# Output products of a two-layer graph attention kernel as seven products of halves, added in place

## The chip, the cores and the metric

The kernel runs on one core of a Trainium2 chip. The metric is the device time of one execution in microseconds (us); lower is better. All data are float32.

## What is computed

The input x holds 128 graphs of 128 nodes with 512 features, adj a boolean adjacency matrix per graph. Two layers follow each other, each an attention over the adjacency with a residual and a layer norm:

```python
# --- layer 0: 4 heads of 64, no norm ahead of the projections ---
q, k, v = x @ Wq, x @ Wk, x @ Wv                    # split into heads
sim  = where(adj, q k^T * 64**-0.5, -float32_max)
x    = layernorm(x + softmax(sim) v @ Wo + bo)
# --- layer 1: 8 heads of 64, layer norm (gamma, beta) ahead of the projections ---
h    = layernorm(x) * gamma + beta
q, k, v = split(h @ w_qkv.T)
sim  = where(adj | eye, q k^T * 64**-0.5, -1e9)
x    = layernorm(x + softmax(sim) v @ w_out.T + b_out)
```

The matrix of attended values that the output product multiplies (called aT here, turned) is 256 wide in layer 0 and 512 wide in layer 1; the output is 512 wide in both.

## The kernel before

**Groups and steps.** The graphs are handled in 64 groups of two ("batches" b = 0 and 1). `step(s)` is a software pipeline written out by hand: at step s it makes the query, key and value products of layer 0 for group s (`product_0`), the softmax of layer 0 for group s - 1, the query and key products of layer 1 for group s - 2 (`p("qk", ...)`), and V and the softmax of layer 1 for group s - 3 (`p("v", ...)`). A step has two halves; half b works on batch b of the softmax groups: `scores` (TensorE), the mask and the row maximum (VectorE), the exponentials (ScalarE), `normalised` (GpSimd), `blocks` (VectorE turns blocks of 32 x 32), a trip through DRAM that completes the transposition (`put`, `fetch`), and `attend` half a step later.

**Order.** The schedule is manual: each engine executes its instructions in the order in which `step` calls the functions, and waits where an operand or a buffer is not ready. `scores` puts the exponentials of its layers into `waiting` and issues layer 0's at once; layer 1's are issued by the next call of `exponentials()`. Copies out of PSUM on ScalarE and adds out of PSUM on VectorE stand in the same queues as the softmax. DMAs are issued from SP, in order too.

**Seven products.** The projections of two batches are already made as one 2 x 2 block product with seven products of halves (the Winograd form of Strassen's scheme) in place of eight. GpSimd makes the sums of the inputs (`sums`), the weights' sums are made once. The seven products go into three accumulators, as this table says (product: accumulator, whether it starts it):

```python
    INTO = {1: ("a", True), 2: ("c", True), 6: ("a", False), 5: ("f", True), 7: ("a", False),
            4: ("a", False), 3: ("f", False)}
```

So products 1, 6, 7 and 4 add into one PSUM bank one after the other, and the bank's partial sums are read out in between: after 1 and 6 by a ScalarE copy (L330, L371), after 7 by a VectorE add (L335, L376), after 4 by a ScalarE copy. A product that adds into the bank waits until the read-out before it is done. Products 5 and 3 share a second bank in the same way.

**Output products.** `residual` makes them for one batch at a time, undivided: two (layer 0) or four (layer 1) chunks of 128 with 512 columns (L493), one VectorE add to the residual (L499), the statistics, and the norm (`norms`, L524, VectorE for both layers) when `flush()` is called. Each float32 matmul shows as two records in the profile.

**PSUM.** Eight banks: five in turn for everything called `mm_tile` (scores take four at a time), and one each for `a`, `a0` and a shared `f`.

Of the kernel before, what the change touches and what calls it, by code (L numbers as in the profile page):

```python
# [18 lines left out]
D = 64  # L19
# [8 lines left out]
def kernel(ctx: ExitStack, tc: tile.TileContext, x, adj, wq, wk, wv, wo, bo,  # L28
# [13 lines left out]
    four = ctx.enter_context(tc.tile_pool(name="four", bufs=4))  # L42
    dram = ctx.enter_context(tc.tile_pool(name="dram", bufs=2, space=bass.MemoryType.DRAM))
    ps_mm = ctx.enter_context(tc.tile_pool(name="ps_mm", bufs=5, space=PSUM))
# [20 lines left out]
    X, M = {}, {}  # L65

    def load(g):
        if g >= NG:
            return
        X[g] = four.tile([P, G, E], F32, tag="x", name=f"x_{g}")  # L70
        M[g] = four.tile([P, G, N], U8, tag="m", bufs=6, name=f"m_{g}")
        nc.sync.dma_start(X[g], x[g * G:(g + 1) * G].rearrange("b n e -> n b e"))
        nc.sync.dma_start(M[g], adj[g * G:(g + 1) * G].rearrange("b i j -> i b j"))
# [8 lines left out]
    mhalf = const.tile([P, 2], F32, name="mhalf")  # L82
# [25 lines left out]

    spare = []
    for tag, n in (("qk1", 4), ("v1", 2), ("xT1", 2), ("xs1", 2)):  # L110
        rows_n = one.tile([P, n, E], F32, tag=tag, name=f"raw_{tag}")
        spare.extend(rows_n[:, i] for i in range(n))

    def load_transposed(dst, src, name, scaled=0):
        rows, cols = src.shape
        raws = []
        for r in range(rows // P):
            if not spare:
                raw = three.tile([P, cols], F32, tag="h", bufs=7, name=f"{name}_{r}")
            else:  # L120
                raw = spare.pop(0)
            nc.sync.dma_start(raw, src[r * P:(r + 1) * P, :])
            raws.append(raw)
# [36 lines left out]
    def weight_sums():  # L160
        for w, ws in ((w1qk, wsqk), (w1v, wsv)):
            for c in range(KH):
                if w is w1qk:
                    b11, b12 = w[:, c, :, 0], w[:, c, :, 1]
                    b21, b22 = w[:, KH + c, :, 0], w[:, KH + c, :, 1]
                else:
                    b11, b12 = w[:, c, 0], w[:, c, 1]
                    b21, b22 = w[:, KH + c, 0], w[:, KH + c, 1]
                t2, t3, t4 = ws[:, 0, c], ws[:, 1, c], ws[:, 2, c]
                nc.vector.tensor_sub(t3, b22, b12)  # L170
                nc.vector.tensor_sub(b12, b12, b11)
                nc.vector.tensor_sub(t2, b22, b12)
                nc.vector.tensor_sub(t4, b21, t2)

    def weight_sums_0():
        b11, b12, b21, b22 = (w0[:, c:c + KH, h].rearrange("p c t f -> p c (t f)")
                              for c in (0, KH) for h in range(2))
        t2, t3, t4 = (ws0[:, i].rearrange("p c t f -> p c (t f)") for i in range(3))
# [4 lines left out]

    weight_sums_0()
    load_transposed(w1, w_qkv, "w_qkv", scaled=INNER[1])
    setup.append(turn_gamma_beta)
    load_transposed(wo1, w_out, "w_out")
    setup.append(weight_sums)

    WO = (wo0, wo1)  # L190
    RATIO, H, XT, QK, V, QKV = {}, {}, {}, {}, {}, {}
# [14 lines left out]
    TURNED, SCR, RAW = {}, {}, {}  # L206

    def turn(l, g, b):
        if not 0 <= g < NG:
            return  # L210
        if b == 0:
            TURNED[l] = one.tile([P, 4, G * KC * 32], F32, tag=f"turned{l}", name=f"turned{l}_{g}")
        src = X[g][:, b] if l == 0 else H[g, b]
        nc.vector.transpose(TURNED[l].rearrange("p a (b c i) -> p a b c i", b=G, c=KC)[:, :, b],
                            src.rearrange("p (c a i) -> p a c i", a=4, i=32))
        if b == G - 1:
            SCR[l] = put(TURNED[l], f"scr{l}_{g}")

    def arrive(l, g):
        if not 0 <= g < NG:  # L220
            return
        RAW[l] = one.tile([P, 4, G, KC, 32], F32, tag=f"raw{l}", name=f"raw{l}_{g}")
        fetch(RAW[l].rearrange("p a b c i -> p a (b c i)"), SCR[l])

    def first_transposed():
        xT = XT[0, 0] = one.tile([P, KC, T], F32, tag="xT0", name="xT0_0")
        for b in range(G):
            pt = mm_tile(f"xt_{b}")
            for c in range(KC):
                nc.tensor.transpose(pt[:, c * N:(c + 1) * N], X[0][:, b, c * P:(c + 1) * P], ident)  # L230
# [26 lines left out]
    def sums(l, g):  # L257
        xT = XT[l, g]
        xs = one.tile([P, 4, KH, N], F32, tag=f"xs{l}", name=f"xs{l}_{g}")
        a = xT.rearrange("p (h c) (b n) -> p b h c n", h=2, b=2)  # L260
# [6 lines left out]
        XS[l, g] = xs  # L267
# [69 lines left out]
    def product_0(g, *which):  # L337
# [5 lines left out]
        for i in which:  # L343
# [10 lines left out]
            elif first:  # L354
                tag = {"a": "a0", "f": "f"}[bank]
                ACC[0, bank] = ps_st.tile([P, 512], F32, tag=tag, name=f"{bank}0_{g}")
# [11 lines left out]
            if i in (1, 5, 6):  # L368
                e = one.tile([P, 512], F32, tag=("e5_0" if i == 5 else f"e{i}"), name=f"e0_{i}_{g}")
                EV[0, i] = e[:, :3 * P]  # L370
# [8 lines left out]
    SM, SUM, PT, AT, XB = {}, {}, {}, {}, {}  # L379
# [56 lines left out]
    def blocks(k):  # L436
# [7 lines left out]
        pT = one.tile([P, 4, sum(HEADS), 32], F32, tag="pT", name=f"pT_{k}")  # L444
# [13 lines left out]
    def attend(k):  # L458
        both = members(k)
        if not both:  # L460
            return
        for l, g, b in both:
            K = HEADS[l] // 2
            pT = PT.pop((l, g, b))
            pm = mm_tile(f"av{l}_{g}_{b}")

            for h in range(HEADS[l]):
                s, kk = h % 2, h // 2
                o = pm[s * D:(s + 1) * D, kk * N:(kk + 1) * N]
                v = QKV[g][:, b, kk, 2, s * D:(s + 1) * D] if l == 0 else V[1, g][:, b, h * D:(h + 1) * D]  # L470
                nc.tensor.matmul(o.rearrange("p (a r) -> p a r", r=32), v, pT[:, :, s * K + kk, :],  # L471
                                 start=True, stop=True)
            AT[l, g, b] = two.tile([P, INNER[l]], F32, tag=f"aT{l}", name=f"aT{l}_{g}_{b}")
            nc.scalar.copy(AT[l, g, b], pm[:, :INNER[l]])  # L474

    def addend(l, k):

        for _, g, b in [m for m in members(k) if m[0] == l]:
            if l == 0:
                xin = X[g][:, b, :]  # L480
            else:
                xin = H.pop((g, b))
                nc.scalar.activation(xin, xin, AF.Copy, scale=RATIO.pop((g, b)))  # L483
            nc.gpsimd.tensor_tensor(xin, xin, (bias0, bias1)[l], op=ALU.add)  # L484
            XB[l, g, b] = xin

    def residual(l, k):
        for _, g, b in [m for m in members(k) if m[0] == l]:
            aT = AT.pop((l, g, b))
            nk = INNER[l] // P  # L490
            pm = mm_tile(f"o{l}_{g}_{b}")
            for c in range(nk):
                nc.tensor.matmul(pm, aT[:, c * P:(c + 1) * P], WO[l][:, c, :],  # L493
                                 start=(c == 0), stop=(c == nk - 1))
            if l == 0:
                y = three.tile([P, E], F32, tag="h", bufs=7, name=f"h_{g}_{b}")
            else:
                y = two.tile([P, E], F32, tag="y", name=f"y_{g}_{b}")
            nc.vector.tensor_add(y, pm, XB.pop((l, g, b)))  # L499
            st = three.tile([P, nc.vector.BN_STATS_DIM], F32, tag="st", name="st")  # L500
            nc.vector.bn_stats(st, y)
            mv = three.tile([P, nc.vector.BN_AGGR_DIM], F32, tag="mv", name=f"mv{l}_{g}_{b}")
            nc.vector.bn_aggr(mv, st)
            n = 2 - l
            ve = three.tile([P, 2], F32, tag="ve", name="ve")
            nc.gpsimd.tensor_scalar_add(ve[:, 0:1], mv[:, 1:2], EPS)  # L506
            if l == 0:


                nc.gpsimd.tensor_scalar(ve[:, 1:2], mv[:, 1:2], 1.0 + EPS, EPS * EPS,  # L510
                                        op0=ALU.mult, op1=ALU.add)
            r = three.tile([P, 2], F32, tag="rstd", name="rstd")
            nc.gpsimd.tensor_tensor(r[:, :n], ve[:, :n], mhalf[:, :n], op=ALU.pow)  # L513
            if l == 0:

                ratio = three.tile([P, 1], F32, tag="ratio", bufs=10, name=f"ratio_{g}_{b}")
                nc.gpsimd.tensor_scalar(ratio, ve[:, 1:2], r[:, 0:1], r[:, 1:2], op0=ALU.mult,
                                        op1=ALU.mult)
                RATIO[g, b] = ratio
            later.append(lambda: norms(l, g, b, y, mv, r))  # L520

    def norms(l, g, b, y, mv, r):
        n = 1 - l
        nc.vector.tensor_scalar(y, y, mv[:, 0:1], r[:, n:n + 1], op0=ALU.subtract, op1=ALU.mult)  # L524
        if l == 0:
            H[g, b] = y
        else:
            nc.sync.dma_start(out[g * G + b], y)


    def step(s):
# [6 lines left out]
        k = 2 * s  # L538
        scores(k)
        addend(0, k - 1)  # L540
        residual(1, k - 2)
        p("qk", 4, g=s - 3)
        exponentials()
        attend(k - 1)
        normalised(k)
        addend(1, k - 1)
        flush()
        turn(0, s + 1, 0)
        turn(0, s + 1, 1)
        product_0(s, 1, 5)  # L550
        p("", g=-1)
        blocks(k)
        arrive(0, s + 1)
        product_0(s, 2, 6)
        p("", g=-1)
        product_0(s, 3)
        residual(0, k - 1)
# [72 lines left out]
```

## Time and profile before

| | |
|---|---|
| median of 3 runs | 2984.99 us (2981.91 to 2985.11) |
| the profiled execution | 2984.46 us, its span 2982.7 us |
| TensorE busy | 2920.0 us, 98% |
| VectorE busy | 1854.0 us, 62% |
| GpSimd busy | 1567.4 us, 53% |
| ScalarE busy | 1334.2 us, 45% |
| granted TensorE clock, mean | 0.994 |

In the profile, PE is TensorE's matmuls, PEld its weight loads (which overlap with them), DVE is VectorE, ACT ScalarE, POOL GpSimd and SP the engine that issues the DMAs. A line of the timeline gives the start, the length, the engine, the line of the kernel, the operation, the tiles (out<-in), the shapes and the number of instructions merged; in brackets the idle time before it and what ended it. Matmuls are pipelined, so the durations of two neighbours overlap and only the difference of two starts is a cost.

### The profile page before, as it was taken

What the parts mean: (1) busy time and instruction counts of PE and PEld (TensorE: products, weight loads), DVE (VectorE), ACT (ScalarE), POOL (GpSimd) and SP (SyncE); (2) the same over time, 40 slices, a digit from 0 to 9 for tenths busy, and PEclk for the clock granted to TensorE, in tenths of its full rate; (3) what the DMA queues carried; (4) which work ended last, traced back from release to release, by engine and by line L of the source; (5) the groups of instructions that cost most, each with busy time, mean ns of one, the idle gap of its engine ahead of it and who ended that gap; (6) DMA issues with size and microseconds to landing.
All of it is one profiled execution on the core that took longest, in us unless ns stands there. A gap on an engine that the chain in (4) does not pass through costs nothing.

```text
span 2982.7 us, 59421 instructions
## 1 busy us (share of the span) xinstructions
PE 2920.0 (98%) x22089; PEld 2402.9 (81%) x22089; DVE 1854.0 (62%) x3291; ACT 1334.2 (45%) x4619; POOL 1567.4 (53%) x2055
## 2 busy tenths in 40 slices
PE   6899999999999999999999999999999999999997
PEld 5788888888888888888888888888888888888865
DVE  4466666666666666666656666666666666666654
ACT  2344444444444444444544444444444444444442
POOL 2455545545545555555555555455455455455543
PEclk8999999999999999999999999999999999999999
DMA  5454544544544544544544545545445445445332
GB/s 170 123 149 129 150 141 127 161 136 124 165 135 125 165 136 127 160 134 134 156 132 140 150 131 147 146 129 153 141 126 161 137 122 168 133 125 163 118 100 89
DMA packets 249136, 414.42 MB, mean 139 GB/s; under 512 B 41608, under 2 KB 181392, under 8 KB 248848
## 3 DMA queue, kind: packets, MB, share of 16 engines
q1 hardware_dynamic: 248848, 410.62, 46.3%
q8 instruction: 175, 2.87, 0.4%
q14 instruction: 113, 0.93, 0.1%
HBM read 209.72 MB, written 200.80 MB: 138 GB/s over the span
## 4 chain that ended last, share of the span: by engine, by line
PE 96%; DVE 1%; DMA 1%; ACT 1%; issue 0%; POOL 0%; SPq 0%; POOLq 0%; DVEq 0%; ACTq 0%
PE o L493 22%; PE qka L304 15%; PE a L361 12%; PE qkf L304 8%; PE va L304 8%; PE sc L400 6%; PE av L471 6%; PE f L361 6%; PE qkc L304 4%; PE vf L304 4%; PE c L361 3%; PE vc L304 2%; ACT sm L424 1%; DMA scrp<-turned 0%; DMA pT<-scrp 0%
## 5 line engine op out<-in xcount | busy, mean ns | idle before, releaser
L424 ACT ACTIVATE sm<-sm,nmax 128x128 f32<-128x128 f32 x1536 | 595.2, 389 | 618.6 <-DVE nmax L415 604.9
L493 PE MATMUL o<-wo,aT 128*128 128x512 f32 x1536 | 713.2, 600 | 10.0 <-ACT aT L474 10.0
L506 POOL TENSOR_SCALAR ve<-mv 128x1 f32<-128x1 f32 x256 | 57.0, 223 | 1133.0 <-DVE rec L432 798.8
L493 PEld LDWEIGHTS o<-wo,aT 128*128 128x128 f32 x1536 | 278.3, 191 | 269.3 <-issue 246.8
L433 POOL TENSOR_TENSOR sm<-sm,rec 128x512 f32<-128x512 f32 (+1 forms) x256 | 397.0, 1561 | 171.9 <-DVE rec L432 171.9
L412 DVE COPY_PREDICATED sm<-m,sc 128x512 f32<-128x512 uint8 (+1 forms) x512 | 271.0, 581 | 29.1 <-POOL sm L410 7.0
L424 ACT ACTIVATION_READ_ACCUMULATOR sm<-sm,nmax 128x1 f32 x1536 | 288.0, 187 | 0.0
L448 DVE STREAM_TRANSPOSE turned<-sm 128x512 f32<-128x512 f32 (+1 forms) x256 | 246.0, 965 | 45.0 <-POOL sm L433 45.0
L304 PE MATMUL qkf<-xs,w 128*128 128x128 f32 x2048 | 249.9, 275 | 0.1
L304 PE MATMUL qka<-xs,wsqk 128*128 128x128 f32 x2048 | 249.6, 275 | 0.0
L415 DVE TENSOR_REDUCE nmax<-sm 128x4 f32<-128x512 f32 (+1 forms) x256 | 244.0, 953 | 8.8
L304 PEld LDWEIGHTS qkf<-xs,w 128*128 128x128 f32 x2048 | 239.0, 192 | 0.6 <-POOL xs L266 0.4
L304 PEld LDWEIGHTS qka<-xs,wsqk 128*128 128x128 f32 x2048 | 239.0, 192 | 0.0
L524 DVE TENSOR_SCALAR h<-h,mv,rstd 128x512 f32<-128x512 f32 x128 | 70.0, 547 | 265.0 <-POOL rstd L513 265.0
L432 DVE RECIPROCAL rec<-total 128x4 f32<-128x4 f32 (+1 forms) x256 | 44.7, 175 | 296.6 <-ACT sm L424 296.6
L266 POOL TENSOR_TENSOR xs<-xT 128x256 f32<-128x256 f32 x256 | 186.0, 727 | 34.4 <-PE w_qkvt L129 14.5
L410 POOL MEMSET sm<- 128x512 f32 (+1 forms) x256 | 181.1, 735 | 1.4 <-DVE turned L448 1.3
L330 ACT COPY ev<-va 128x256 f32<-128x256 f32 x128 | 47.6, 372 | 298.7 <-PE va L304 298.7
L513 POOL TENSOR_TENSOR rstd<-ve,mhalf 128x2 f32<-128x2 f32 (+1 forms) x256 | 165.9, 648 | 21.3
L330 ACT COPY eqk<-qka 128x512 f32<-128x512 f32 x128 | 75.1, 587 | 214.4 <-PE qka L304 214.4
L484 POOL TENSOR_TENSOR h<-h,bias 128x512 f32<-128x512 f32 x128 | 162.7, 1271 | 7.0 <-ACT h L483 6.9
L484 POOL TENSOR_TENSOR x<-x,bias 128x512 f32<-128x512 f32 x128 | 162.2, 1267 | 0.0
(122 smaller groups left out, 5825.5 us busy)
## 6 DMA issues: line engine op xcount, KB each, us to landing
scrp<-turned SPq DMA_DIRECT2D x124, 768.0 KB, 3.3
pT<-scrp SPq DMA_DIRECT2D x496, 192.0 KB, 4.0
scr<-turned SPq DMA_DIRECT2D x127, 512.0 KB, 2.7
raw<-scr SPq DMA_DIRECT2D x508, 128.0 KB, 3.0
x<-in_x_dram SPq DMA_DIRECT2D x64, 512.0 KB, 4.2
out_dram<-y SPq DMA_DIRECT2D x128, 256.0 KB, 2.0
m<-in_adj_dram SPq DMA_DIRECT2D x64, 32.0 KB, 4.0
scrp<-turned SPq DMA_DIRECT2D x4, 512.0 KB, 3.2
```

Source lines behind the costliest of these rows:

```text
L266: nc.gpsimd.tensor_tensor(o, a0, a1, op=op)
L304: nc.tensor.matmul(o, lhsT, rhs, start=first and n == 0, stop=n == len(todo) - 1, skip_group_check=True)
L361: nc.tensor.matmul(acc[:, t * P:(t + 1) * P], lhsT, rhs, start=first and n == 0, stop=n == len(todo) - 1, skip_group_check=True)
L400: nc.tensor.matmul(ps[h % 2][:, h // 2, :], q_, k_, start=True, stop=True)
L410: nc.gpsimd.memset(sm, (NEG0, NEG1)[l])
L412: nc.vector.copy_predicated(sm[:, s], mask[:, None, :].to_broadcast([P, K, N]), ps[s][:, :K, :])
L415: nc.vector.tensor_reduce(nmax, sm, AX.X, ALU.max, negate=True)
L424: nc.scalar.activation(sm[:, s, k, :], sm[:, s, k, :], AF.Exp, bias=nmax[:, s, k:k + 1], accum_out=total[:, s, k:k + 1])
L433: nc.gpsimd.tensor_tensor(sm, sm, rec[:, :, :, None].to_broadcast([P, 2, K, N]), op=ALU.mult)
L448: nc.vector.transpose(t[:, :, lo:hi, :], sm)
L484: nc.gpsimd.tensor_tensor(xin, xin, (bias0, bias1)[l], op=ALU.add)
L493: nc.tensor.matmul(pm, aT[:, c * P:(c + 1) * P], WO[l][:, c, :], start=(c == 0), stop=(c == nk - 1))
```

## The change

- The output products become seven products of halves for both batches of a group in one go (`out_product`), each with 256 columns: one chunk (layer 0) or two chunks (layer 1). They use the same table `INTO`. After each product VectorE adds what stands in the accumulator, in place, to the quarter of one tile per group (`R`, which holds x, then the residual, then the result), so there are seven adds of 256 columns per group and layer.
- GpSimd makes the four sums of the attended values (`out_sums`); the sums of the output weights are made once (`weight_sums_out`).
- `attend` works on both batches of a group, a step after their softmax, with one copy for layer 0 and two for layer 1. Layer 1 runs at s - 4; there is one more step, and no code after the last one.
- The bias is added to both batches at once. The statistics stay per batch, the roots are taken once per group, and the norm of layer 1 moves from VectorE to ScalarE.
- PSUM: four banks in turn, and one each for `a`, `a0`, `f` and `f0`. The probabilities have two buffers.
- The order inside `step` is new, as the diff shows.

```diff
-    ps_mm = ctx.enter_context(tc.tile_pool(name="ps_mm", bufs=5, space=PSUM))
+    ps_mm = ctx.enter_context(tc.tile_pool(name="ps_mm", bufs=4, space=PSUM))
...
+    def out_product(l, g, *which):
+        if not 0 <= g < NG:
+            return
+        aT, so = AT[l, g], SO[l, g]
+        hk = INNER[l] // P // 2
+        w, ws = WO[l], WSO[l]
+        EH = E // 2
+        for i in which:
+            left = {1: aT[:, 0, :hk], 2: aT[:, 0, hk:], 3: so[:, 3], 4: aT[:, 1, hk:], 5: so[:, 0],
+                    6: so[:, 1], 7: so[:, 2]}[i]
+            right = {1: w[:, :hk, :EH], 2: w[:, hk:, :EH], 3: w[:, hk:, EH:], 4: ws[:, 2],
+                     5: w[:, :hk, EH:], 6: ws[:, 0], 7: ws[:, 1]}[i]
+            bank, first = INTO[i]
+            if first and bank == "c":
+                ACC["o", bank] = mm_tile(f"oc{l}_{g}")
+            elif first:
+                ACC["o", bank] = ps_st.tile([P, 512], F32, tag=(bank, f"{bank}0")[l], name=f"o{bank}{l}_{g}")
+            acc = ACC["o", bank][:, :EH]
+            for c in range(hk):
+                nc.tensor.matmul(acc, left[:, c], right[:, c], start=first and c == 0, stop=c == hk - 1,
+                                 skip_group_check=True)
+            b, h = {1: (0, 0), 2: (0, 0), 6: (0, 1), 3: (0, 1), 5: (1, 1), 7: (1, 1), 4: (1, 0)}[i]
+            part = R[g][:, b, h * EH:(h + 1) * EH]
+            nc.vector.tensor_add(part, acc, part)
...
+    def attend(s):
+
+        for l, g in ((0, s - 2), (1, s - 4)):
...
+    def out_sums(l, g):
+        if not 0 <= g < NG:
+            return
+        K = HEADS[l] // 2
+        so = SO[l, g] = one.tile([P, 4, K // 2, N], F32, tag=("so", "xs0")[l], name=f"so{l}_{g}")
+        halves_sums(so, AT[l, g].rearrange("p b (h c) n -> p b h c n", h=2))
...
+    def norms_0(g, mv, root):
+        for b in range(G):
+            nc.vector.tensor_scalar(R[g][:, b], R[g][:, b], mv[:, b, 0:1], root[:, 1, b:b + 1],
+                                    op0=ALU.subtract, op1=ALU.mult)
+
+    def norms_1(g, shift, root):
+        for b in range(G):
+            nc.scalar.activation(R[g][:, b], R[g][:, b], AF.Identity, bias=shift[:, b:b + 1],
+                                 scale=root[:, 0, b:b + 1])
+        nc.sync.dma_start(out[g * G:(g + 1) * G].rearrange("b n e -> n b e"), R[g])
```

The body of `step` after the change, in full (it replaces the one before):

```python
        k = 2 * s
        if s:
            load(s + 1)
        scores(k)
        addend(0, s - 2)
        p("qk", 4, g=s - 3)
        product_0(s, 1)
        exponentials()
        attend(s)
        out_sums(0, s - 2)
        normalised(k)
        product_0(s, 5)
        p("", g=-1)
        product_0(s, 2)
        addend(1, s - 4)
        p("", g=-1)
        out_product(0, s - 2, 1, 5, 2, 6)
        product_0(s, 6)
        p("", g=-1)
        out_product(0, s - 2, 3)
        stats(0, s - 2, 0)
        out_product(0, s - 2, 7)
        blocks(k)
        product_0(s, 3)
        p("", g=-1)
        out_product(0, s - 2, 4)
        stats(0, s - 2, 1)
        product_0(s, 7)
        p("", g=-1)
        flush()
        turn(1, s - 2)
        probs_arrive(k)
        product_0(s, 4)
        arrive(1, s - 2)
        k += 1
        scores(k)
        out_sums(1, s - 4)
        p("v", 1, 5, g=s - 3)
        exponentials()
        p("v", 2, 6, g=s - 3)
        out_product(1, s - 4, 1)
        p("v", 3, 7, g=s - 3)
        normalised(k)
        out_product(1, s - 4, 5, 2)
        p("v", 4, g=s - 3)
        finish(s - 2)
        turn(0, s + 1)
        out_product(1, s - 4, 6)
        blocks(k)
        out_product(1, s - 4, 3)
        stats(1, s - 4, 0)
        out_product(1, s - 4, 7)
        arrive(0, s + 1)
        probs_arrive(k)
        p("qk", 1)
        out_product(1, s - 4, 4)
        stats(1, s - 4, 1)
        p("qk", 5)
        p("qk", 2)
        in_order(s + 1)
        flush()
        p("qk", 6)
        p("qk", 3, 7)
```

## The prediction

> **What bounds the kernel now.** I read the page's busy shares first, then its chain of waits, then one full step in order of time on each engine, and last the places where TensorE stood still. Of the page, the busy line and the chain by line:
>
> ```profile
> PE 2920.0 (98%) x22089; PEld 2402.9 (81%) x22089; DVE 1854.0 (62%) x3291; ACT 1334.2 (45%) x4619; POOL 1567.4 (53%) x2055
> ...
> PE o L493 22%; PE qka L304 15%; PE a L361 12%; PE qkf L304 8%; PE va L304 8%; PE sc L400 6%; PE av L471 6%; PE f L361 6%; PE qkc L304 4%; PE vf L304 4%; PE c L361 3%; PE vc L304 2%; ACT sm L424 1%; DMA scrp<-turned 0%; DMA pT<-scrp 0%
> ```
>
> TensorE's own queue is the bound: it is busy 98% of the span, and the output products (L493), which the change rewrites, carry the largest share of the chain. Fewer matmul columns are worth time only if TensorE never waits for an eviction. The timeline of TensorE over one step:
>
> ```profile
> 1003.47 0.71 PE L400 MATMUL sc<-qkv 64*128 64x128 f32 x8
> ...
> 1021.40 1.03 PE L304 MATMUL vf<-w,xs 128*128 128x256 f32 x4
> 1022.27 1.03 PE L304 MATMUL vc<-w,xT 128*128 128x256 f32 x4
> 1023.13 1.03 PE L304 MATMUL va<-wsv,xs 128*128 128x256 f32 x4
> ...
> 1024.95 0.71 PE L400 MATMUL sc<-qkv 64*128 64x128 f32 x8
> ...
> 1027.46 3.60 PE L493 MATMUL o<-wo,aT 128*128 128x512 f32 x8
> 1030.89 1.03 PE L304 MATMUL va<-wsv,xT 128*128 128x256 f32 x4
> ...
> 1034.75 1.88 PE L493 MATMUL o<-wo,aT 128*128 128x512 f32 x4
> 1036.47 1.05 PE L361 MATMUL a<-xT,ws 128*128 128x128 f32 x8
> ...
> 1048.62 0.71 PE L400 MATMUL sc<-qkv 64*128 64x128 f32 x8
> ```
>
> Only start-to-start differences count here, since matmul records overlap. One step (one group) takes 1048.62 - 1003.47 = 45.15 us. Now look at what stands between two products that share an accumulator. Product 7 of V starts at 1026.49, and product 4, which adds into the same bank, at 1030.89; between them lie the 3.43 us of an output product. The same holds for layer 0's products 7 and 4, with the output product of 1034.75 between. VectorE and ScalarE show why that filling is needed. VectorE:
>
> ```profile
> 1028.97 1.22 DVE L415 TENSOR_REDUCE nmax<-sm 128x8 f32<-128x1024 f32 x1
> 1030.11 0.41 DVE L335 TENSOR_TENSOR v<-va,ev 128x256 f32<-128x256 f32 x1
> ...
> 1034.95 0.56 DVE L376 TENSOR_TENSOR qkv<-a,e 128x384 f32<-128x384 f32 x1
> ```
>
> ScalarE:
>
> ```profile
> 1027.65 0.40 ACT L424 ACTIVATE sm<-sm,nmax 128x128 f32<-128x128 f32 x1 [3.08 <-DVE m L407]
> ...
> 1030.29 0.40 ACT L424 ACTIVATE sm<-sm,nmax 128x128 f32<-128x128 f32 x1 [0.99 <-DVE nmax L415]
> ...
> 1033.38 0.35 ACT L332 COPY v<-va 128x256 f32<-128x256 f32 x1
> ```
>
> The bank is read out late, because VectorE is in order and busy with the softmax: product 7 ends near 1027.5, its eviction (L335) starts at 1030.11, product 4 at 1030.89. The output products were the cover. ScalarE is just as ordered: layer 0's exponentials start 2.70 us after the score products (1024.95), layer 1's eight at 5.34 us, and whatever copy stands behind them waits until 1033.38, that is 8.43 us.
>
> **The change, part by part.** Fewer columns: a 512-column output record costs 3.43 / 8 = 0.43 us, a 256-column record of V 0.865 / 4 = 0.216 us, so halving the width loses nothing per column. Before, a group has 2 x 1.72 + 2 x 3.43 = 10.30 us of output products. After, layer 0 has 7 products of 2 records and layer 1 7 of 4: 14 x 0.216 + 28 x 0.216 = 9.07 us. TensorE's work falls by 1.22 us a step, from 45.15 to 43.93, or 78 us over 64 groups.
>
> What the other engines gain or lose in busy time: VectorE loses four 512-column adds (0.67 to 0.69, L499) and two norms of layer 1 (0.89, L524), 4.5 us, and gets fourteen 256-column adds at the 0.385 to 0.415 us of the V adds (L335), 5.7 us. ScalarE gets two norms (not shown with a bias at this shape; 0.73 us of L483 to twice the 0.59 of L252; I take 0.73, the same shape). GpSimd gets eight sums: four of 256 columns at 0.73 us (L266), four of 128 columns that no row shows (between the 0.22 of L506 and 0.73; 0.45 by the step from 0.73 at 256 to 1.27 at 512, L484). Its bias add of 1024 columns lies between 2.08 (L433) and 2 x 1.27; I take 2.3. The power over four columns lies between 0.72 (two columns, L513) and 1.0 (two more at the 0.14 by which two exceed one); I take 1.0. In sum VectorE rises from 28.7 to about 30 us a step, GpSimd from 24.5 to about 27, ScalarE from 20.8 to 22; none becomes the bound by its sum. One score buffer fewer costs nothing: the twelve allocations of a step take the four buffers in turn, and the tightest, V's product 2, takes the first score tile, wanted 3.3 us after the scores and copied out by 2.7. Loads, attended probabilities and raw rows move on SP: the probabilities' fetch now stands behind the put of layer 1's turned rows (issued at about 24 us of the step), lands near 30, and is read in the next step, over 20 us later; load(s + 1) lands 4 us into the step and is read at 35. The output's put waits for ScalarE near 47, with only the next load behind it. Hidden as well are the sums of outputs (ready at 9.5 us and on, their first reader at 11.1). If one of these covers were gone, its price would be its own latency, 3 to 4 us a step.
>
> **Where the waits come.** I walk a step in the new order with these durations; 0 is the start of its first score products. TensorE: scores to 1.54, qk 4 to 3.4, product_0 1 to 4.9, attend to 7.9, product_0 5 and 2 to 10.7, out 1, 5, 2, 6 to 12.45, product_0 6 to 13.9, out 3 and 7 to 14.75, product_0 3 to 16.1, out 4 to 16.55, product_0 7 to 17.9. ScalarE keeps up (exponentials end at 8.4, both copies of the attention outputs by 9.9). VectorE has, from the end of out 3 at 14.4, in program order: add 0.45, stats 0.8, add of out 7 0.4, the two transposes 1.9, product_0 3 0.5, out 4 0.45, stats 0.85, product_0 7 0.55: 5.9 us, to 20.35. Product_0 4 adds into that bank and now directly follows product_0 7, so TensorE stands from 17.9 to 20.4: **2.5 us**.
>
> Second half, 0 at its scores (21.8 of the step). VectorE first waits for GpSimd's roots (20.0 plus 0.3, 0.3, 1.0), does the norms (1.1) and the turn (1.35), so it starts on the scores at 2.25 instead of 0.8. Exponentials of layer 0 run 3.85 to 5.4; the copy of V's product 1, which used to be issued before the scores, now stands behind them, to 5.75. V's product 6 adds into that bank; TensorE reaches it at 4.1 and starts at 5.85: **1.7 us**. Then the exponentials of layer 1 run 6.75 to 9.85 and the copy of product 6 stands behind those, to 10.2. Product 7 is reached after product 6, out 1 and product 3, at 8.45, and starts at 10.3: **1.85 us**. At the end, out 4 of layer 1 waits for the add of out 7, which follows transposes and stats: VectorE is at 18.65, TensorE at 18.1: **0.6 us**. Behind all that, TensorE has only qk products, which the others have time to serve.
>
> Sum: 43.93 + 2.5 + 1.7 + 1.85 + 0.6 = 50.6 us a step, 5.43 more than now. About 62 of the steps have all of it: 337 us. The fill and drain get one more, nearly empty step but lose a tail; I take nothing. Against the profiled execution (2984.46 us, span 2982.7; the median of the runs is 2984.99) that gives 3321 us.
>
> **The clock.** Near the end of the trace TensorE stood 2.55 us, and the 4 records that followed took 3.50 us instead of 1.88. Its timeline and the window:
>
> ```profile
> 2906.01 3.50 PE L493 MATMUL o<-wo,aT 128*128 128x512 f32 x4 [2.55 <-ACT aT L474]
> ```
> ```profile
> 2906.00:2909.30 3.30, 3.29 (x4) 1.51 (x5) 1.51 (x2) 1.06 (x2) 3.29 (x2) 0.53 0.24 82
> ```
>
> The granted clock was 0.53 there. Three other gaps of 2.3 to 2.6 us (before 2865.57, 2923.62 and 2957.92) cost under 0.4 us each. One in four at 1.6 us, at the one gap of a step that is as long, makes 0.4 us, 25 us in all: 3346, told as 3345. The Trainium skill ("TensorE: Matmul & The Clock Gate", Part 1: The HAM clock gate) says that the clock falls to half after an idle window of about 3.4 us; by that none of my waits would cost clock, and the sum would stay 3321; the row at 2906 shows a loss after a shorter gap.
>
> **The rivals.** Short waits: if VectorE is never behind, what the order alone forces remains: 0.7 for product_0 4 (the 0.56 us add and its signals), and 0.3 + 1.8 for V's products, with layer 1's exponentials done at 8.4 after the scores. That is 2.8 us, 46.7 a step, 3083 us. The busy sums speak for it, VectorE's walk against it. Faster: if the waits sum to under 1.22 us a step the saved columns decide, down to 2984.5 - 78 = 2906 us. It needs the copies of V's products 1 and 6 to come before the exponentials, or those to be done by 7 us after the scores; the ScalarE rows (eight of them starting at 5.34, ended at 8.4) speak against it. Colder: if every wait of 2.5 us halves the clock as at 2906, 62 x 1.6 = 100 us come on top of 3321: 3420 us. That seven products save nothing, because narrower ones cost more per column, is excluded by the 0.216 and 0.43.
>
> **How the numbers follow.** Forecast 0.72, short waits 0.12, colder 0.08, faster 0.06, waits that just eat the gain 0.02. Measurement can tell about 0.2% from no change. The range runs from 3120 (half way out to the short waits) to 3440 (the colder case); it leaves out the faster cases and most of the short waits. The forecast's own range is 3230 to 3400, by about 1.5 us a step on the waits, for adds and pool rows that may be off.
>
> **What would show it.** Right: scores 50 to 51 us apart; TensorE's busy share near 87%; in the list of waits, TensorE's layer-0 product (a) on VectorE's qkv with about 150 us in 62 times, and its V product (va) on ScalarE's ev with about 220 us in 124; output records at 0.216 us. Wrong: those waits under 75 us together, or scores under 45 us apart; or a wait for GpSimd's sums or a DMA as the largest.

## The result, and the profile after

The change makes the kernel slower: 3400.93 us (median of 4 runs, 3399.23 to 3401.1) against 2984.71 us, a ratio of 1.1396 (95% interval 1.1376 to 1.1415). The forecast was 3345 us in a range of 3120 to 3440. The profiled execution took 3401.1 us, its span 3399.2 us.

The busy line and the chain by engine, from the page of the changed kernel, and below them the chain of the kernel before:

```profile
PE 2996.0 (88%) x23241; PEld 2708.4 (80%) x23241; DVE 1987.4 (58%) x3811; ACT 1412.5 (42%) x4683; POOL 1728.5 (51%) x2247
...
PE 55%; DVE 24%; ACT 9%; issue 5%; DMA 3%; POOL 2%; SPq 1%; ACTq 0%; DVEq 0%; POOLq 0%
```
```profile
PE 96%; DVE 1%; DMA 1%; ACT 1%; issue 0%; POOL 0%; SPq 0%; POOLq 0%; DVEq 0%; ACTq 0%
```

TensorE carried 96% of the chain before; now VectorE and ScalarE carry a third of it. No engine became the bound by its sum. What TensorE waited for (us in total, times, longest):

```profile
PE va L312 <- ACT ev L338: 177.7, 96, 6.5
PE a L368 <- DVE qkv L382: 117.6, 64, 2.6
PE oa L404 <- DVE r L408: 24.0, 67, 1.5
```

These are the waits that the prediction named: V's products behind ScalarE's copies, layer 0's product 4 behind VectorE's add of product 7, and layer 1's last output product (4) behind VectorE's add of output product 7. In one step TensorE's timeline shows each in its place:

```profile
1052.50 1.05 PE L368 MATMUL a<-xs,ws 128*128 128x128 f32 x8
...
1055.87 1.16 PE L368 MATMUL a<-xT,ws 128*128 128x128 f32 x8 [1.87 <-DVE qkv L382]
...
1058.94 1.13 PE L312 MATMUL va<-w,xT 128*128 128x256 f32 x4
1059.91 1.03 PE L312 MATMUL vf<-w,xs 128*128 128x256 f32 x4
1060.90 1.13 PE L312 MATMUL vc<-w,xT 128*128 128x256 f32 x4
1063.97 1.13 PE L312 MATMUL va<-wsv,xs 128*128 128x256 f32 x4 [1.94 <-ACT ev L338]
1064.94 1.03 PE L404 MATMUL oa<-wo,aT 128*128 128x256 f32 x4
...
1068.65 1.13 PE L312 MATMUL va<-wsv,xs 128*128 128x256 f32 x4 [1.82 <-ACT ev L338]
...
1072.21 1.03 PE L404 MATMUL oa<-wso,so 128*128 128x256 f32 x4
1073.08 1.03 PE L404 MATMUL of<-wo,so 128*128 128x256 f32 x4
...
1077.07 1.13 PE L404 MATMUL oa<-wso,aT 128*128 128x256 f32 x4 [0.32 <-DVE r L408]
```

In brackets stands how long TensorE was idle, counted from the modelled end of the product before, and what ended it. Counted by starts a wait costs 0.3 to 0.4 us more: from 1060.90 to 1064.94 are 4.04 us for eight records that take 1.73 without a wait. The step's scores of its second half start at 1057.40. ScalarE's timeline over the same stretch says why V's products wait:

```profile
1062.02 0.40 ACT L456 ACTIVATE sm<-sm,nmax 128x128 f32<-128x128 f32 x1 [4.03 <-DVE nmax L447]
...
1063.57 0.35 ACT L338 COPY ev<-va 128x256 f32<-128x256 f32 x1
...
1065.16 0.40 ACT L456 ACTIVATE sm<-sm,nmax 128x128 f32<-128x128 f32 x1 [0.97 <-DVE nmax L447]
...
1068.26 0.35 ACT L338 COPY ev<-va 128x256 f32<-128x256 f32 x1
```

Product 1 of V had started on TensorE at 1058.94 and took 0.97 us; its copy (1063.57) stands behind layer 0's four exponentials, which waited 4.03 us for a row maximum. The copy of product 6 (1068.26) stands behind layer 1's eight. And VectorE's timeline says why the row maximum is late:

```profile
1055.29 0.53 DVE L382 TENSOR_TENSOR qkv<-a,e 128x384 f32<-128x384 f32 x1
1057.08 2.23 DVE L571 TENSOR_SCALAR r<-r,mv,root 128x512 f32<-128x512 f32 x2 [1.27 <-POOL root L555]
1059.23 1.29 DVE L223 STREAM_TRANSPOSE turned<-r 128x512 f32<-128x512 f32 x2
1060.45 0.73 DVE L444 COPY_PREDICATED sm<-m,sc 128x256 f32<-128x256 uint8 x2
```

First the add that product 4 waits for, then 1.27 us of waiting for GpSimd's roots, then the norms and the turn; the scores are copied out from 1060.45 on, 3.05 us after TensorE began them. The prediction's walk through a step had put that at 2.25 us, with 1.1 us for the norms; they took 2.23. But in this the step shown is not typical. In 45 of 56 steps of the middle (from the second scores of step 5 to those of step 61) the two norms take 1.34 us, in 11 they take 2.23. In one of the 45 the second scores start at 1003.95 and are copied out 2.15 us later:

```profile
1003.62 1.34 DVE L571 TENSOR_SCALAR r<-r,mv,root 128x512 f32<-128x512 f32 x2 [1.27 <-POOL root L555]
1004.88 1.28 DVE L223 STREAM_TRANSPOSE turned<-r 128x512 f32<-128x512 f32 x2
1006.10 0.73 DVE L444 COPY_PREDICATED sm<-m,sc 128x256 f32<-128x256 uint8 x2
```

GpSimd fills the next score tiles (sm) beside the norms, first in the typical step, then in the one shown above:

```profile
1004.16 1.69 POOL L442 MEMSET sm<- 128x512 f32 x2
```
```profile
1057.62 1.41 POOL L442 MEMSET sm<- 128x512 f32 x2
```

The two instructions merged in each line tell the cases apart: in the typical step the second norm ends 0.28 us behind the first memset (and the second memset is the longer one), in the other 0.28 us behind the second.

A fourth thing is not in the list of waits. Two neighbouring windows (length, busy time and instructions of PE, PEld, DVE, ACT and POOL, then granted clock, DMA share, GB/s):

```profile
1011.30:1014.70 3.40, 1.25 (x7) 0.77 (x5) 0.57 (x3) 3.27 (x17) 0.00 (x0) 1.00 1.01 193
1014.70:1018.10 3.40, 3.40 (x8) 2.74 (x9) 0.93 (x4) 0.00 (x0) 0.76 (x1) 0.50 0.00 0
```

After 3.4 us in which TensorE was busy for 1.25, it worked for 3.4 us at half clock. Over the whole span the granted clock was 0.961, where it had been 0.994.

The bill, from the starts of the scores in both timelines: steps 5 to 63 took 51.36 us each (45.15 before), together 366 us more; the steps ahead of them took 25 us more, the drain behind them 25 us more. 366 + 50 = 416, the difference of the spans.

### The profile page after: what moved, and what is told of

Read it like the earlier page. It is cut to its first block, busy times and chain, and to the rows that moved or that the text cites. A ratio compares the mean times of both kernels' runs of the same rounds, so it can differ in the third digit from the quotient of the medians.

```text
span 3399.2 us, 62735 instructions
## 1 busy us (share of the span) xinstructions
PE 2996.0 (88%) x23241; PEld 2708.4 (80%) x23241; DVE 1987.4 (58%) x3811; ACT 1412.5 (42%) x4683; POOL 1728.5 (51%) x2247
## 4 chain that ended last, share of the span: by engine, by line
PE 55%; DVE 24%; ACT 9%; issue 5%; DMA 3%; POOL 2%; SPq 1%; ACTq 0%; DVEq 0%; POOLq 0%
PE qka L312 10%; ACT sm L456 7%; PE a L368 6%; PE oa L404 5%; PE av L507 5%; PE qkf L312 5%; PE va L312 5%; DVE turned L480 5%; PE of L404 4%; PE sc L432 4%; DVE sm L444 4%; DVE st L539 4%; DVE nmax L447 3%; DVE r L408 3%; PE f L368 3%
## 5 line engine op out<-in xcount | busy, mean ns | idle before, releaser
L275 POOL TENSOR_TENSOR so<-aT 128x128 f32<-128x128 f32 (+1 forms) x256 | 155.8, 609 | 433.5 <-ACT aT L512 433.5
L312 PE MATMUL va<-wsv,xs 128*128 128x256 f32 x512 | 156.5, 432 | 178.5 <-ACT ev L338 177.7
L528 POOL TENSOR_TENSOR r<-r,bias 128x1024 f32<-128x1024 f32 x128 | 301.7, 2357 | 5.8 <-ACT r L527 5.8
L408 DVE TENSOR_TENSOR r<-oa,r 128x256 f32<-128x256 f32 x512 | 212.0, 414 | 140.4 <-PE oa L404 121.9
L312 PEld LDWEIGHTS va<-wsv,xs 128*128 128x128 f32 x512 | 93.5, 202 | 232.1 <-ACT ev L338 221.2
L404 PE MATMUL of<-wo,so 128*128 128x256 f32 x768 | 223.7, 403 | 3.0 <-POOL so L275 3.0
L379 ACT COPY qkv<-a 128x384 f32<-128x384 f32 x64 | 30.6, 478 | 466.0 <-PE a L368 450.4
L404 PE MATMUL oa<-wso,so 128*128 128x256 f32 x768 | 211.8, 385 | 0.4 <-DVE r L408 0.4
L548 POOL TENSOR_SCALAR ve<-mv 128x2 f32<-128x2 f32 x128 | 28.1, 220 | 308.9 <-DVE mv L540 308.9
L539 DVE BATCH_NORM_STATS2 st<-r 128x6 f32<-128x512 f32 x256 | 177.9, 695 | 8.8
```

Source lines behind the costliest of these rows:

```text
L275: nc.gpsimd.tensor_tensor(o, a0, a1, op=op)
L312: nc.tensor.matmul(o, lhsT, rhs, start=first and n == 0, stop=n == len(todo) - 1, skip_group_check=True)
L404: nc.tensor.matmul(acc, left[:, c], right[:, c], start=first and c == 0, stop=c == hk - 1, skip_group_check=True)
L408: nc.vector.tensor_add(part, acc, part)
L528: nc.gpsimd.tensor_tensor(R[g], R[g], (bias0, bias1)[l][:, None, :].to_broadcast([P, G, E]), op=ALU.add)
L539: nc.vector.bn_stats(st, R[g][:, b])
```

## The experiments

The theory: TensorE's waits come from where the evictions stand in the in-order queues of VectorE and ScalarE. Its rival: seven adds per group and layer, and the sums, are too much for VectorE and GpSimd in any order.

**e1: layer 1's exponentials behind the copy of V's product 6.**

```diff
-        exponentials()
         p("v", 2, 6, g=s - 3)
+        exponentials()
```

> Layer 1's exponentials are issued behind the copy of V's product 6 instead of ahead of it. If that copy's place in ScalarE's queue makes the third wait (1.8 us a step), that wait goes and nothing takes its place: about 62 x 1.8 = 112 us less, 3290 us, and down to 3245 if the spells of half clock that follow these waits go with it. If VectorE's load, not the order, sets the pace, the wait turns up at a later product and the time stays within 20 us of 3401.

Measured: 3225.0 us, 1.0807 (1.0789 to 1.0825) of the kernel before, 176 us less than the change alone. TensorE's waits:

```profile
PE a L368 <- DVE qkv L382: 117.5, 64, 2.6
PE va L312 <- ACT ev L338: 45.7, 36, 1.9
```

The waits of V's products fell from 177.7 to 45.7 us in all, and the wait for product 7 did not change: the third wait was the place of one call. The gain exceeds the 112 us of the wait, and the 156 us of the lower figure. Counted by starts the third wait had cost 2.4 us a step, not the 1.9 in the brackets, and the half clock fell too, from 2.96 us a step to 1.71 in the mean of the 56 steps of the middle.

**e2: layer 0's product 4 behind V's products 1 and 5.**

```diff
-        product_0(s, 4)
         arrive(1, s - 2)
...
         p("v", 1, 5, g=s - 3)
+        product_0(s, 4)
         exponentials()
```

> Layer 0's product 4 is moved behind the scores and V's products 1 and 5, so that 3.3 us of TensorE's work lie between it and product 7. If the waits are independent of each other, the first one (1.9 us a step) goes: 62 x 1.9 = 117 us less, 3284 us. If the first two waits are one lag, that of VectorE's chain of adds, statistics, norms and turns at the end of the first half, TensorE only arrives earlier at V's product 6 and waits there for 4 us instead of 1.9: 3380 to 3420 us.

Measured: 3397.25 us, 1.1377 (1.1360 to 1.1394). TensorE's waits:

```profile
PE va L312 <- ACT ev L338: 177.6, 116, 6.5
PE vc L312 <- DVE sm L444: 81.8, 62, 3.4
```

The wait for product 7 is gone from the list and nothing is gained. TensorE came earlier to V's product 2, whose bank of PSUM is the first score tile, and waited there for VectorE to copy it out (1.3 us in each of 62 steps), then at V's product 6, where the wait rose from 0.8 to 1.9 us a step in the mean of the 56 steps. So the 1.9 us that went at product 4 came back as 2.4 at the next two products: the first two waits are one lag. At V's product 7 the wait fell from 1.9 to 0.7 us, so that TensorE was idle for 0.6 us a step less at these places; but half clock rose from 2.96 to 4.02 us a step, and the step stayed at 51.35 us. The buffer taken from the scores, priced at nothing, is where a TensorE that comes earlier meets that lag first.

**e3: the idle time filled.** Seven matmuls on the identity, ahead of products 4, V 6 and V 7, in steps 4 to 63; nobody reads them.

```diff
+        fill("a", 7)
         product_0(s, 4)
...
+        fill("b", 7)
+        p("v", 6, g=s - 3)
...
+        fill("c", 7)
+        p("v", 7, g=s - 3)
```

> Seven 128-column matmuls that nobody reads (1.56 us) are put into each of the three long waits; the order of all else stays, and the output is the same. If the idle time itself halves the clock, the spells of half clock (about one a step, 3.4 us each) vanish: some 50 x 1.7 = 85 us less, about 3320 us, granted clock above 0.99. If the spells lie inside waits anyway and cost nothing, the time stays at 3401 or rises by what the filling overruns, up to 3420.

Measured: 3376.25 us, 1.1310 (1.1293 to 1.1327): 24.7 us less than the change, with 4.7 us more work on TensorE in a step. In the 56 steps of the middle no spell is left, where there had been 2.96 us of half clock a step; the granted clock of the span rose to 0.987, the rest of the loss lying in fill and drain. So the spells come from the idle time, and they cost time; but a step took 50.93 us instead of 51.35, less than a third of the 1.5 us that 2.96 us at half speed lose. A slower TensorE then waits less: the steps with a spell waited 5.02 us, those without 5.67. The price expected here, 85 us, had left that out. As the filling may overrun, 25 us is a lower bound of it.

**e4: another order of the same operations.** The attention of the outputs stands directly behind the first scores, so that its copies pass layer 1's exponentials; layer 0's output products come ahead of most of product_0; V's products 5 and 1 lie between layer 0's products 3, 7 and 4; no copy that TensorE waits for stands behind exponentials.

```diff
         scores(k)
         addend(0, s - 2)
-        p("qk", 4, g=s - 3)
-        product_0(s, 1)
-        exponentials()
         attend(s)
         out_sums(0, s - 2)
+        p("qk", 4, g=s - 3)
+        exponentials()
+        product_0(s, 1)
...
+        addend(1, s - 4)
+        product_0(s, 6)
         p("", g=-1)
         flush()
         turn(1, s - 2)
         probs_arrive(k)
+        product_0(s, 3)
+        p("v", 5, g=s - 3)
+        product_0(s, 7)
+        p("v", 1, g=s - 3)
         product_0(s, 4)
...
```

> All operations of the changed kernel, in another order: the outputs' attention ahead of qk 4, layer 0's output products ahead of most of product_0, V's products 5 and 1 between layer 0's 3, 7 and 4, no ScalarE copy that TensorE waits for behind exponentials. If order alone made the loss, TensorE's waits fall under 0.5 us a step and the saved columns show: 2900 to 2930 us. If seven adds of 256 columns per layer are more than VectorE can serve in time, whatever the order, the time stays above 3050.

Measured: 3205.05 us, 1.0740 (1.0724 to 1.0756): 196 us less than the change, but above the 3050 us that were expected if VectorE can't serve seven adds in any order. By its number the run speaks for the rival. Its waits name something else: V's are gone, but one is longer than ever:

```profile
PE a L368 <- DVE qkv L382: 214.0, 64, 3.5
```

VectorE's timeline of one step, and what GpSimd did meanwhile:

```profile
1532.84 4.92 DVE L571 TENSOR_SCALAR r<-r,mv,root 128x512 f32<-128x512 f32 x2
```
```profile
1532.91 2.35 POOL L528 TENSOR_TENSOR r<-r,bias 128x1024 f32<-128x1024 f32 x1
1535.21 1.41 POOL L442 MEMSET sm<- 128x512 f32 x2
```

The two norms take 4.92 us (4.06 and 0.93), though the shortest of their kind is 0.53 us in this run. The first ends 0.28 us behind the last of three GpSimd instructions in a row, the bias add and two memsets. The new order had put GpSimd's bias add beside them.

**e6: that one call moved away.** (The call `addend` holds two ScalarE scalings too, which move with the bias add.)

```diff
         out_sums(0, s - 2)
+        addend(1, s - 4)
         p("qk", 4, g=s - 3)
...
-        addend(1, s - 4)
         product_0(s, 6)
```

> The kernel of e4_new_order with one call moved: GpSimd's bias add for layer 1 (2.35 us) is issued right after the sums of layer 0's outputs and no longer behind the roots, where it ran beside VectorE's norms of layer 0 (4.92 us for the two in that step, 1.1 us where VectorE works alone). If GpSimd's large operations hold the norms up, these shrink to about 2.6 us and TensorE's wait for layer 0's product 7 from 3.5 to about 1.3 us: 62 x 2.2 = 136 us less, 3070 us, and down to 3040 with the spells of half clock behind them. If the norms are slow for a reason of their own, the time stays within 20 us of 3205.

Measured: 2995.64 us, 1.0039 (1.0024 to 1.0054), 209 us less than e4. The norms, and GpSimd beside them:

```profile
1522.56 2.19 DVE L571 TENSOR_SCALAR r<-r,mv,root 128x512 f32<-128x512 f32 x2
```
```profile
1522.61 1.42 POOL L442 MEMSET sm<- 128x512 f32 x2
```

The norms fall from 4.92 to 2.19 us (2.6 expected), and TensorE's wait from 214.0 to 50.5 us, 0.8 us a step (1.3 expected). The rest of the 209 us is the clock: e4 had 2.09 us of half clock a step, and a mean step of 48.53 us where its steps without a spell took 47.73; in e6 no spell is left in the 56 steps, more than the expectation allowed for. With every operation on the engine where the changed kernel has it, e6 is 0.4% slower than the kernel before, not 14%: that the adds and sums are too much in any order is refuted by this. The Trainium skill ("SBUF — State Buffer", SBUF: two separate sides) says that VectorE and GpSimd share one pair of ports as an exclusive lock: of a GpSimd instruction and a VectorE instruction that needs the pair, the one that starts first holds it for its whole length. The norm of e4 that starts beside the bias add and ends 0.28 us behind GpSimd's third instruction looks like that. Which of the two engines comes next the page doesn't say; in the changed kernel it went both ways, 45 times against 11.

**e5: the norms of layer 0 on ScalarE too** (GpSimd makes the bias for them, as it does in layer 1), with layer 0's product 3 ahead of the turn and V's product 2 ahead of layer 0's product 4.

```diff
-            nc.vector.tensor_scalar(R[g][:, b], R[g][:, b], mv[:, b, 0:1], root[:, 1, b:b + 1],
-                                    op0=ALU.subtract, op1=ALU.mult)
+            nc.scalar.activation(R[g][:, b], R[g][:, b], AF.Identity, bias=shift[:, b:b + 1],
+                                 scale=root[:, 1, b:b + 1])
...
         flush()
+        product_0(s, 3)
         turn(1, s - 2)
         probs_arrive(k)
-        product_0(s, 3)
...
-        p("v", 1, g=s - 3)
+        p("v", 1, 2, g=s - 3)
         product_0(s, 4)
```

> As e6_bias_add_early, and the norms of layer 0 go to ScalarE like those of layer 1 (0.8 us each), layer 0's product 3 stands ahead of the turn, and V's product 2 ahead of layer 0's product 4. If VectorE's place behind GpSimd was the last thing that TensorE waited for, its waits fall under 0.5 us a step: 62 x 44.2 us and the ends, 2910 to 2950 us, faster than before the change by 1 to 2.5%. If seven adds per layer are too many for VectorE in any order, it stays above 3000.

Measured: 2950.35 us (2948.75 to 2951.31), 0.9885 (0.9868 to 0.9901) of the kernel before: 1.15% faster, the first version that beats it, 0.35 us above the upper end of what was expected. TensorE's largest waits, and its middle by windows:

```profile
PE av L507 <- DMA pT<-scrp: 20.3, 5, 12.4
PE oa L404 <- DVE rec L464: 11.2, 63, 0.2
```
```profile
250.00:2720.00 2470.00, 2458.05 (x20151) 2258.05 (x20151) 1588.72 (x3183) 1304.55 (x4185) 1510.46 (x2065) 1.00 0.49 144
```

The largest wait is one of the fill; the other is 0.18 us a step. TensorE is busy 99.5% of the middle at full clock, a step takes 44.29 us. The seven products, adds and sums are all still there. Three things changed at once, and no run tells their shares apart. Of the 50 us that 59 steps save against the kernel before, the fill and the drain take 17 back.

**e8: e5 with product 2 of each output made twice**, as many columns as eight products have.

```diff
-            for c in range(hk):
...
+            for _ in range(2 if i == 2 else 1):
+                for c in range(hk):
...
```

> As e5_norms_on_scalar, with product 2 of each output made twice (the second run overwrites the first, the result is the same), so that TensorE does as many columns as eight products would need: 0.43 + 0.865 = 1.3 us more a step. If TensorE is the bound of that order, the time rises by about 62 x 1.3 = 80 us over it; if waits still set it, by less than 30.

Measured: 3018.9 us, 1.0117 (1.0102 to 1.0132), 68.5 us over e5; a step takes 1.10 us more. So the eighth product, the one thing that the scheme saves, is worth about 69 us once TensorE is the bound, of the 80 expected. What it would be worth in the changed kernel's own order no run shows.

## Why the prediction was right

**Columns.** A record of 256 output columns starts every 0.216 us in the changed kernel too (0.865 us from 1072.21 to 1073.08 for four of layer 1). The saving of 1.22 us a step was expected from that; e8 gives 1.10 for nearly the same columns. It is real, and small beside the waits.

**Waits.** The four places and their causes were right, and so nearly were their sizes. The walk counted by starts; so counted, less what the same products take at their usual spacing, the four waits cost 2.2, 1.7, 2.4 and 0.6 us in the six of the 56 steps that had no half clock (2.5, 1.7, 1.85 and 0.6 forecast), 6.8 us together where the walk summed 6.65. These six steps took 50.59 us each, the walk 50.6. The third wait was set too short, the first too long, and these two errors nearly cancel, which is luck. In the brackets the idle time of these steps is 5.67 us, in the mean of all 56 it is 5.1. For the waits and the spells of half clock are in part two names of one time: in 23 of the 56 steps the second wait is not there at all, and in each of these TensorE ran at half clock between the second scores and V's product 6 and came there later. By the signs set beforehand: scores were 51.36 us apart (50 to 51 forecast, so just missed), TensorE's share was 88% (87), the wait for product 7 made 117.6 us in 64 times (150 in 62), V's waits 177.7 in 96 (220 in 124). The forecast's own narrower range, 3230 to 3400 us, was missed by 1 us.

**VectorE's lag.** The scores were copied out 2.17 us after their start in the mean of the 56 steps, where the walk had 2.25. The norms, 1.1 us by rows in which VectorE worked alone, took 1.51 us in the mean (1.34 or 2.23, by GpSimd's memsets); what the rest took made up for that. The profile of the kernel before had held the hint, the norms of layer 1 (L524) with a mean of 0.89 us against 0.55 of layer 0's.

**The clock.** 25 us were set for it, from one gap in four that cost 1.6 us. In 50 of the 56 steps lay a spell or a part of one, and the steps took 51.35 us in the mean where those without one took 50.59: 0.76 us, some 45 us in all (an estimate, as the two sorts of steps may differ in more than the clock); e3 gives 25 at least. The idle window of about 3.4 us that the Trainium skill ("TensorE: Matmul & The Clock Gate", Part 1: The HAM clock gate) gives would have made it nothing; here a TensorE that was idle for a little over half of such a window lost the clock in the next.

**Fill and drain** were set at nothing and cost 50 us, of which the forecast's three edge steps (it counted 62 full ones, not 59) held about 17. Ahead of step 5 TensorE's idle time rose from 37 to 58 us and the time at half clock from 24 to 55 us; behind the start of step 64 they rose from 19 to 35 and from 14 to 42 us. The longest of the waits that are new are in the changed kernel's first 110 us, where TensorE waits 12.2 us for the turned input of layer 0's group 2 and 9.4 for layer 1's first, and in the drain, where V's product 7 waits 6.5 and 6.4 us behind exponentials. No run tests the ends by themselves. This term (33 us) and the clock's (21) make the 55 us that the forecast was short.

**The rivals.** "Short waits" failed where it was said to: VectorE is behind in each step. "Faster" was excluded by the right row. "Colder" had the mechanism and too high a price; that its 3420 us lie nearer to the result than the forecast's 3345 is luck, as most of the difference is fill and drain. What the forecast didn't see is how little of the loss belongs to the change: the same operations in another order, with two norms on another engine, are 1.15% faster than the kernel before.

## What to carry to other kernels

When a kernel is bound by TensorE and its products add into one bank, the question is not how long an eviction takes, but what stands ahead of it in its engine's queue, and how much other work TensorE has between the two products. Walk one step engine by engine; here that came within 2% of the step measured. In the trace read several steps before you take a row for typical: one of the norms above was twice as long in one step of five as in the rest. If a wait goes when a call moves, look whether it turns up at the next product before counting it as a gain: e2 removed one and gained nothing. A new order is also a new neighbourhood: check what GpSimd does beside each VectorE norm.

## What the runs showed of the hardware

- Half clock follows a stretch that is half idle, not only a wholly idle one. Every stretch of one clock between two changes, in all nine traces, is a whole multiple of 3.413 us long. Cut into such windows, the middle of the changed kernel and of e1, e2 and e4 has 161 windows at full clock followed by a spell; TensorE was idle in all of them for 1.78 us or more. Of over 3000 other windows at full clock, some 60 reach 1.75 us, and none 2.0. In e6, where no window of the middle reaches 0.85, no spell occurs there.
- A VectorE norm of 128x512 (one tensor in SBUF, in place) took 0.53 us alone and up to 4.07 beside GpSimd's bias add and memsets (e4). Where a norm was held up, it ended 0.28 us behind the end of a GpSimd instruction, in all of some 310 cases (64 in the kernel before, where it is L524, 64 in the changed one, 122 in e4, 64 in e6). The mask's maximum (L439, two tensors in SBUF) went from 0.28 to a mean of 0.71 us in the changed kernel, where GpSimd's sums or its bias add run beside it.
- ScalarE's norm with a bias and a scale per partition takes 0.81 us for 128x512, GpSimd's power over four columns 1.02 us, its sum of 128 columns 0.46 us: close to the values taken between rows (0.73, 1.0 and 0.45).
